# Expert logits computed with tokens on the partitions instead of with the tokens along the free axis

## The chip, the core and the metric

The kernel runs on one core of a Trainium2 chip. A core has five engines that run their own instruction streams and meet at semaphores: TensorE (PE: matrix products; its weight loads are listed apart as PEld), VectorE (DVE), ScalarE (ACT), GpSimd (POOL) and SyncE (SP, which issues the DMAs here). On-chip data lies in SBUF, 128 partitions wide; TensorE writes its products to PSUM, which the kernel uses as eight banks of 128 x 512 four-byte numbers, and DVE or ACT carry them on from there. The metric is the device time of one execution in microseconds; lower is better.

## What is computed

The input `x` is 16 sequences of 512 tokens with 256 channels. It is normalised, and the output is `x` plus a multi-query attention (16 heads of width 16, one shared key and value head) plus a mixture of six small experts, both of the normalised tokens. The change lies in the expert part. Cut to what matters, with `E = 6` experts, `L = 100` learned tokens each, rank `R = 16`, `C = 256` channels:

```python
logits = x @ w_gate                              # [n, E]
top_vals, top_idx = lax.top_k(logits, 1)
gates = zeros.at[arange(n)[:, None], top_idx].set(softmax(top_vals))
tokens = einsum('elr,erc->elc', A, B)            # [E, 100, C], rank 16
attn = einsum('nc,elc->nel', x, tokens) * C ** (-0.5)
attn = softmax(attn, axis=-1)                    # over the 100 learned tokens
val = einsum('elc,dc->eld', tokens, wt_w) + wt_b
delta_f = einsum('nel,eld->ned', attn[:, :, 1:], val[:, 1:, :])
delta = (einsum('ned,cd->nec', delta_f + x[:, None, :], wd_w) + wd_b) * scale[0]
combined = sum(exp(delta) * gates[:, :, None], axis=1)
out = feats + log(where(combined == 0, eps, combined))
```

One expert is open for a token (its gate is one), so the kernel computes only that one: the logits of a token against the 100 learned tokens of its own expert are `A_e (B_e x)`. `B x` for all six experts is 96 numbers a token (`ER = 96`); those of the five closed experts are multiplied by zero; and one product over the 96 rows with `A` then gives the 100 logits.

## The kernel before

The work is cut into 16 batches, one for each sequence (`NB = 16`, `T = 512` tokens). A batch's work is cut into some 310 jobs, each one method of the class `Batch`: `load`, `stats`, `norm`, `trans` (transposes of the normalised tokens), `q`, `e`, `kv` (projections), `amax` (a first pass over the attention logits that finds the maxima, on 128 x 512 tiles `pA`), `score`, `exp` and `pv` (the attention proper: logits `ps`, their exponentials `P`, the products `po`), `wo` (the output projection `py`) and the expert jobs. No order is left to a scheduler: each job has a written-out place in one of four tables (`FIRST`, `SECOND`, `MIDDLE` for batches 2 to 14, `LAST`), a batch's table is shifted by `PERIOD = 131072` units for each batch, all jobs of all batches are sorted by place (line 1175), and each engine executes its instructions in that order. So a place sets only who comes before whom, and the jobs of two or three batches are interleaved. `OTHER` and `KINDS` (lines 361 and 449) say which engine does a job.

PSUM banks come from a ring of eight (`Ring`, line 396): a job that makes a product takes the bank that has been free longest, and the job that reads it gives it back; TensorE must then wait until the bank's last reader is done.

Products that must be nearly exact in four bytes are made by `mm3` (line 424): each operand is split into a rounded part and the rest, both of type `float32r` (FR), and three products are accumulated: first with first (line 426), first with rest (427), rest with first (428). The first operand given to a product is the stationary one, which a weight load brings into the array; the second one is moved through it, one column after another.

The expert jobs that the change touches, in the order in which a batch executes them:

- `z` (line 674): `B x`, 96 rows by 512 tokens, in a bank `pz`; `z_ev` multiplies it by the mask of the open expert into `zu`; `z_split` splits it into the pair `self.Z`, two tiles of 96 x 512 (the profile calls them `F`).
- `s` (line 694): `mm3` with `aT` (the pair that holds the transposed `A`, 96 rows by 100 columns) as the stationary operand and `Z`, 512 columns wide, as the moving one. The 100 x 512 logits, tokens along the free axis, go to a bank `pS`.
- `s_ev` (line 698): ACT copies the bank to an SBUF tile `fs` in every batch (`KINDS` names ACT first for it and `OTHER` has no entry for it).
- `s_t` (line 704): four transposes of 100 x 128 of `fs` into one bank `pT`. The tokens then lie on the partitions, 100 logits in each quarter of the bank.
- `s_max` (line 709): DVE takes the maximum of the 100 logits of each token and subtracts it, reading `pT` twice; `s_exp` (716) on ACT, `p_t` (719) transposes back, `p_split`, `g` and the rest follow.

In a middle batch the places are `z_split` -152096, `s` -145485, `s_ev` -142958, `s_t` -137276, `s_max` -130921; between `s` and `s_t` stand jobs of other parts, among them `amax`, `score` and the eight transposes of the next tokens.

Of the kernel before, what the change touches and what calls it, by code (L numbers as in the profile page):

```python
# [8 lines left out]
F32 = mybir.dt.float32  # L9
# [59 lines left out]
    "z": -780943,  # L69
    "z_ev": -576470,  # L70
    "z_split": -548352,
    "s": -521686,
    "s_ev": -494550,
    "s_max": -431082,
    "s_exp": -359417,
    "p_split": -293663,
# [38 lines left out]
    "wo": (215817, 215842),  # L115
    "wo_ev": (216596, 217780),
    "store": 224560,
    "s_t": -481591,
    "p_t": -315138,
    "fin3": (40264, 22382),  # L120
    "fin4": (74229, 86847),
# [23 lines left out]
    "z": -324174,  # L145
    "z_ev": -309855,
    "z_split": -270323,
    "s": -218678,
    "s_ev": -209993,
    "s_max": -170106,  # L150
    "s_exp": -121203,
    "p_split": -114910,
# [37 lines left out]
    "wo": (177597, 177346),  # L190
    "wo_ev": (182932, 182876),
    "store": 185963,
    "s_t": -182999,
    "p_t": -116683,
    "fin3": (85629, 17491),
    "fin4": (103962, 139179),
# [23 lines left out]
    "z": -157899,  # L220
    "z_ev": -156539,
    "z_split": -152096,
    "s": -145485,
    "s_ev": -142958,
    "s_max": -130921,
    "s_exp": -125321,
    "p_split": -117179,
# [37 lines left out]
    "wo": (174065, 177554),  # L265
    "wo_ev": (176557, 183488),
    "store": 192519,
    "s_t": -137276,
    "p_t": -119609,
    "fin3": (74999, 108824),  # L270
    "fin4": (77905, 117792),
# [23 lines left out]
    "z": -158149,  # L295
    "z_ev": -154439,
    "z_split": -142977,
    "s": -125619,
    "s_ev": -123150,
    "s_max": -113232,  # L300
    "s_exp": -111784,
    "p_split": -87249,
# [46 lines left out]
    "tail_wo2": (2206909, 1942360, 2812099, 2282694),  # L349
    "tail_ev": (2218028, 1993855, 3175267, 2301583),  # L350
    "tail_store": (2237425, 2218212, 3336794, 2419839),
    "s_t": -118987,
    "p_t": -89378,
    "fin3": (390985, 455221),
    "fin4": (721831, 1298561),
# [18 lines left out]
def tile_kernel(ctx, tc, x, Wq, bq, Wkv, bkv, Wo, bo, A, B, w_gate, wt_w, wt_b, wd_w, wd_b, scale, out):  # L374
    nc = tc.nc
    ctx.enter_context(tc.manual_schedule())
    NB, T, C = x.shape
    E, L, R = A.shape
# [13 lines left out]
    sb2 = ctx.enter_context(tc.tile_pool(name="sb2", bufs=2))  # L392
# [29 lines left out]
    bank = banks.take  # L422

    def mm3(ps, a, b, first=True, last=True):
        (a1, a2), (b1, b2) = a, b
        nc.tensor.matmul(ps, a1, b1, start=first, stop=False)  # L426
        nc.tensor.matmul(ps, a1, b2, start=False, stop=False)  # L427
        nc.tensor.matmul(ps, a2, b1, start=False, stop=last)  # L428
# [10 lines left out]
    def split(engs, p1, p2, src):  # L439
        affine(engs[0], p1, src)  # L440
        engs[1].tensor_tensor(p2, src, p1.bitcast(F32), ALU.subtract)  # L441

    def at(pair, *idx):
        return (pair[0][idx], pair[1][idx])

    ALL = slice(None)
# [6 lines left out]
        ("p_split", (AV, VV, AV)),  # L453
        ("tail_split", (AV, VV, PV)),
        ("prep_kv prep_kv2", (nc.gpsimd, nc.vector, nc.vector)),
        ("trans_ev q_ev s_ev m_ev", (nc.scalar, nc.vector, nc.vector)),
        ("amax_ev", (nc.scalar, nc.vector, nc.vector)),
        ("e_ev ks_ev mask_ev o_ev tail_o", (nc.vector, nc.scalar, nc.scalar)),
    )
# [2 lines left out]
    def copy(eng, dst, src):  # L462
        (eng.copy if eng is nc.scalar else eng.tensor_copy)(dst, src)

    def cols(t, n=128):
        return slice(t * n, t * n + n)


    class Batch:
# [220 lines left out]
        def z_split(self):  # L690
            self.Z = self.pair(ER, "Z")
            split(self.eng("z_split"), self.Z[0], self.Z[1], self.zm)

        def s(self):
            p = self.pb[("s", 0)] = bank(f"pS{self.b}")
            mm3(p[:L], aT, self.Z)

        def s_ev(self):
            p = self.last(("s", 0))
            self.fs = self.tile(sb2, [L, T], F32, "fs")  # L700
            copy(self.eng("s_ev"), self.fs, p[:L])


        def s_t(self):
            p = self.pb[("st", 0)] = bank(f"pT{self.b}")
            for t in range(4):
                nc.tensor.transpose(p[:, t * 128 : t * 128 + L], self.fs[:, cols(t)], ident[:L, :L])

        def s_max(self):
            p = self.last(("st", 0)).rearrange("p (t l) -> p t l", t=4)[:, :, 0:L]  # L710
# [284 lines left out]
    ident = const.tile([128, 128], F32, name="ident")  # L995
# [7 lines left out]
    def fr_pair(shape, name):  # L1003
        return (const.tile(shape, FR, name=name + "1"), const.tile(shape, FR, name=name + "2"))
# [24 lines left out]
    aT = fr_pair([ER, L], "aT")  # L1029
# [174 lines left out]
```

## Time and profile before

| | |
|---|---|
| median of three runs | 927.23 us (926.7 to 928.15) |
| the profiled execution's own time | 929.27 us |
| its span, first to last instruction | 927.5 us |
| mean granted TensorE clock | 0.984 of full speed |

The profiled execution is one run with the profiler on. Its span is what the rows of the profile add up to; its own time is 1.8 us more, for what lies before the first and after the last instruction.

The rows of the groups that the change touches, summed over the span (a "busy" time counts each moment once; a mean is how long one instruction is in flight, and as products are pipelined, two that follow each other start closer together than that):

| instructions | engine | count | busy us | mean ns |
|---|---|---|---|---|
| products `pS<-F,aT` (lines 426, 427, 428) | PE | 16 each | 7.4, 6.2, 6.3 | 464, 389, 395 |
| copy `fs<-pS` 100 x 512 (line 463) | ACT | 16 | 9.4 | 591 |
| transposes `pT<-ident,fs` 100 x 128 (line 707) | PE | 64 | 8.6 | 258 |
| maximum `sm<-pT` 128 x 400 (line 712) | DVE | 16 | 9.1 | 566 |
| difference `es<-pT,sm` 128 x 400 (line 714) | DVE | 16 | 9.2 | 574 |

For comparison, the other products in `float32r` have 512 (`pq`, `pz`, `pG`, `pA`, `ps`), 294 (`pe`), 258 (`pM`) and 256 (`py`) moving columns, and the operands of the transposes (`pt`, `pk`, `pP`, `pT`, `pMt`) are four bytes wide with 100 or 128 moving columns.

### The profile page before, as it was taken

The page shows a single profiled execution, that of the slowest core. Times are in us where ns is not written, and L with a number is a line of the kernel's source. Part 1 is how long each engine was busy: PE and PEld are TensorE (multiplying, and loading weights), DVE is VectorE, ACT ScalarE, POOL GpSimd, SP SyncE. Part 2 cuts the span into 40 slices and gives each one's busy share as a digit, 9 for nine tenths or more (in the row PEclk, how much of TensorE's full clock was granted, in tenths as well). Part 3 has the DMA queues.
Part 4 walks back from the last instruction along what each step waited for, and adds up shares of the span by engine and source line. Part 5 has one row for each costly group of instructions (what it writes and reads, how often), then busy time and mean ns, then how long its engine had stood idle before and what let it go on. Part 6 is the DMA issues. An engine that isn't in the chain of part 4 may idle for free.

```text
span 927.5 us, 18665 instructions
## 1 busy us (share of the span) xinstructions
PE 913.6 (99%) x5994; PEld 483.4 (52%) x5997; DVE 792.0 (85%) x2049; ACT 777.4 (84%) x1715; POOL 613.7 (66%) x842
## 2 busy tenths in 40 slices
PE   8999999999999999999999999999999999999997
PEld 5655445555645555554545555454555545444443
DVE  6798898899898999989898998989888888887743
ACT  4688878889899888989898888989888898897775
POOL 3484746767677776767767676776767677465364
PEclk9989999999999999999999999999999999999989
DMA  3311122231213223131322313132231312222001
GB/s 105 92 36 34 51 49 71 56 77 50 71 40 82 59 68 76 44 71 44 72 59 72 72 44 73 42 72 58 71 73 42 72 43 51 59 51 69 27 26 36
DMA packets 92253, 54.74 MB, mean 59 GB/s; under 512 B 19323, under 2 KB 88188, under 8 KB 92156
## 3 DMA queue, kind: packets, MB, share of 16 engines
q1 hardware_dynamic: 92156, 53.55, 23.3%
q8 instruction: 48, 0.79, 0.4%
q14 instruction: 49, 0.40, 0.1%
HBM read 17.89 MB, written 8.90 MB: 29 GB/s over the span
## 4 chain that ended last, share of the span: by engine, by line
PE 90%; DVE 4%; DMA 2%; ACT 1%; issue 1%; POOL 1%; SPq 0%; POOLq 0%; ACTq 0%; DVEq 0%
PE po L837 26%; PE pA L782 17%; PE ps L821 17%; PE pe L426 2%; PE py L426 2%; PE pq L426 2%; PE pe L428 2%; PE pe L427 2%; PE pq L427 2%; PE py L428 2%; PE pq L428 2%; PE py L427 2%; PE pt L559 1%; DVE rl L795 1%; PE pk L654 1%; DVE M L797 1%
## 5 line engine op out<-in xcount | busy, mean ns | idle before, releaser
L829 ACT ACTIVATE P<-ps 128x512 f32<-128x512 f32 x1024 | 547.5, 614 | 63.4 <-PE ps L821 59.4
L797 DVE TENSOR_REDUCE M<-pA 128x1 f32<-128x512 f32 x661 | 428.6, 683 | 55.3 <-PE pA L782 47.8
L837 PE MATMUL po<-P,vt 128*32 128x512 f32 x2048 | 265.0, 603 | 0.1
L821 PE MATMUL ps<-qst,kst 50*128 50x512 f32 x1024 | 227.7, 443 | 2.5 <-DMA qst<-mt 0.9
L782 PE MATMUL pA<-kst,qst 48*128 48x512 f32 x1024 | 216.6, 444 | 1.4 <-DVE es L714 0.6
L821 PEld LDWEIGHTS ps<-qst,kst 50*128 50x128 f32 x1024 | 108.2, 186 | 114.6 <-DVE M L795 20.5
L782 PEld LDWEIGHTS pA<-kst,qst 48*128 48x128 f32 x1024 | 100.9, 187 | 119.5 <-ACT P L829 20.6
L794 ACT ACTIVATE rl<-pA 128x256 f32<-128x256 f32 x363 | 129.1, 392 | 35.7 <-PE pA L782 32.3
L795 DVE CUSTOM_DVE_ANT_0 rl<-pA,rl 128x256 f32<-128x256 f32 x363 | 141.1, 418 | 20.9 <-ACT rl L794 19.3
L837 PEld LDWEIGHTS po<-P,vt 128*32 128x32 f32 x2048 | 45.0, 108 | 92.5 <-issue 69.7
L758 POOL TENSOR_SCALAR g<-dl 128x512 f32<-128x512 f32 x32 | 61.7, 1930 | 34.7 <-DVE dl L750 33.2
L880 POOL TENSOR_TENSOR oq<-ao,rb 128x512 f32<-128x512 f32 x31 | 40.2, 1298 | 58.8 <-DMA rb<-dr 26.7
L441 POOL TENSOR_TENSOR F<-zu,F 96x512 fp32r<-96x512 f32 (+1 forms) x32 | 41.0, 1281 | 15.1 <-ACT F L433 11.4
L764 POOL TENSOR_SCALAR dl<-dl 128x512 f32<-128x512 f32 x32 | 47.8, 1492 | 2.4
L437 POOL TENSOR_SCALAR F<-zu 98x512 fp32r<-98x512 f32 (+1 forms) x29 | 18.4, 635 | 45.7 <-DVE zu L688 42.5
L441 POOL TENSOR_TENSOR qs<-qf,qs 128x512 fp32r<-128x512 f32 x32 | 41.2, 1288 | 10.9 <-ACT qs L433 8.6
L765 POOL TENSOR_TENSOR w<-dl,w 128x512 f32<-128x512 f32 x32 | 41.2, 1289 | 2.7
L426 PE MATMUL pe<-e1w,X 128*128 128x294 f32 x128 | 41.9, 327 | 0.0
L441 POOL TENSOR_TENSOR O<-oq,O 128x512 fp32r<-128x512 f32 x31 | 39.8, 1285 | 2.5
L769 POOL TENSOR_TENSOR g<-g,bob 128x512 f32<-128x512 f32 x32 | 41.1, 1284 | 0.2
L773 POOL TENSOR_TENSOR w<-g,w 128x512 f32<-128x512 f32 x32 | 41.1, 1287 | 0.1
L635 POOL TENSOR_TENSOR oh<-e,mx 128x24 f32<-128x24 f32 x16 | 3.7, 231 | 55.2 <-ACT P L829 37.5
(209 smaller groups left out, 1503.6 us busy)
## 6 DMA issues: line engine op xcount, KB each, us to landing
qst<-qs SPq DMA_DIRECT2D x384, 64.0 KB
rb<-dr SPq DMA_DIRECT2D x31, 256.0 KB
xt<-in_L_attn_x SPq DMA_DIRECT2D x15, 512.0 KB
out<-y SPq DMA_DIRECT2D x15, 512.0 KB
qst<-mt SPq DMA_DIRECT2D x128, 8.0 KB
dc<-os SPq DMA_DIRECT2D x62, 8.0 KB
dr<-dc SPq DMA_DIRECT2D x62, 8.0 KB
xt<-in_L_attn_x SPq DMA_DIRECT2D x4, 128.0 KB
```

What stands on the lines that cost most here:

```text
L426: nc.tensor.matmul(ps, a1, b1, start=first, stop=False)
L427: nc.tensor.matmul(ps, a1, b2, start=False, stop=False)
L428: nc.tensor.matmul(ps, a2, b1, start=False, stop=last)
L441: engs[1].tensor_tensor(p2, src, p1.bitcast(F32), ALU.subtract)
L758: nc.gpsimd.tensor_scalar(self.g1[:, two], self.dl[:, two], EXP_ZERO, LOG_EPS - EXP_ZERO, ALU.is_lt, ALU.mult)
L782: nc.tensor.matmul(p, self.qst[g][rows, h], self.kst[rows, keys], start=True, stop=True)
L794: nc.scalar.activation(rl, p[:, HT:], AF.Relu)
L795: nc.vector.tensor_tensor_reduce(rl, p[:, 0:HT], rl, 1.0, NEG, ALU.add, ALU.max, accum_out=mx)
L797: nc.vector.tensor_reduce(mx, p, AX.X, ALU.max)
L821: nc.tensor.matmul(p, self.kst[rows, cols(c)], self.qst[hp // 4][rows, :, cols(hp % 4, 32)], start=True, stop=True)
L829: nc.scalar.activation(self.P_[k][:, u], banks.give(self.ps.pop(i)), AF.Exp)
L837: nc.tensor.matmul(self.po[n][32 * j : 32 * j + 32], lv, self.P_[2 * w + j // 2][:, j % 2], start=c == 0, stop=c == 3)
```

## The change

`s` and `s_t` become one job that keeps the name `s` and stands at the places that `s_t` had. For each quarter of the tokens it makes the same three products with the operands exchanged: 128 columns of `Z` are now the stationary operand, and `aT`, 100 columns wide, is the moving one. The result has the tokens on the partitions and is written straight to where the transposes put it, so `s_max` and all that follows is as before. `s_ev`, its copy, the tile `fs`, the bank `pS` and the transposes are gone. `Z` is read later than before: at the place of `s_t`.

```diff
@@ the four tables; here MIDDLE @@
-    "s": -145485,
-    "s_ev": -142958,
+    "s": -137276,
...
-    "s_t": -137276,
@@ KINDS @@
-        ("trans_ev q_ev s_ev m_ev", (nc.scalar, nc.vector, nc.vector)),
+        ("trans_ev q_ev m_ev", (nc.scalar, nc.vector, nc.vector)),
@@ class Batch @@
         def s(self):
-            p = self.pb[("s", 0)] = bank(f"pS{self.b}")
-            mm3(p[:L], aT, self.Z)
-
-        def s_ev(self):
-            p = self.last(("s", 0))
-            self.fs = self.tile(sb2, [L, T], F32, "fs")
-            copy(self.eng("s_ev"), self.fs, p[:L])
-
-
-        def s_t(self):
             p = self.pb[("st", 0)] = bank(f"pT{self.b}")
             for t in range(4):
-                nc.tensor.transpose(p[:, t * 128 : t * 128 + L], self.fs[:, cols(t)], ident[:L, :L])
+                mm3(p[:, t * 128 : t * 128 + L], at(self.Z, ALL, cols(t)), aT)
```

The places in the other three tables change in the same way (`FIRST` -521686 to -481591, `SECOND` -218678 to -182999, `LAST` -125619 to -118987).

More of the change, by code (lines that the diff above doesn't have):

```diff
@@ L71 @@
     "z_split": -548352,
-    "s": -521686,
-    "s_ev": -494550,
+    "s": -481591,
     "s_max": -431082,
@@ L117 @@
     "store": 224560,
-    "s_t": -481591,
     "p_t": -315138,
@@ L147 @@
     "z_split": -270323,
-    "s": -218678,
-    "s_ev": -209993,
+    "s": -182999,
     "s_max": -170106,
@@ L192 @@
     "store": 185963,
-    "s_t": -182999,
     "p_t": -116683,
@@ L297 @@
     "z_split": -142977,
-    "s": -125619,
-    "s_ev": -123150,
+    "s": -118987,
     "s_max": -113232,
@@ L351 @@
     "tail_store": (2237425, 2218212, 3336794, 2419839),
-    "s_t": -118987,
     "p_t": -89378,
```

## The prediction

> **What bounds the kernel now.** I read the page's busy times first, then the chain of work that ended last, then the costliest groups with their idle time, then stretches of one batch each.
>
> ```profile
> PE 913.6 (99%) x5994; PEld 483.4 (52%) x5997; DVE 792.0 (85%) x2049; ACT 777.4 (84%) x1715; POOL 613.7 (66%) x842
> ...
> PE 90%; DVE 4%; DMA 2%; ACT 1%; issue 1%; POOL 1%; SPq 0%; POOLq 0%; ACTq 0%; DVEq 0%
> ...
> L829 ACT ACTIVATE P<-ps 128x512 f32<-128x512 f32 x1024 | 547.5, 614 | 63.4 <-PE ps L821 59.4
> L797 DVE TENSOR_REDUCE M<-pA 128x1 f32<-128x512 f32 x661 | 428.6, 683 | 55.3 <-PE pA L782 47.8
> L837 PE MATMUL po<-P,vt 128*32 128x512 f32 x2048 | 265.0, 603 | 0.1
> L821 PE MATMUL ps<-qst,kst 50*128 50x512 f32 x1024 | 227.7, 443 | 2.5 <-DMA qst<-mt 0.9
> L782 PE MATMUL pA<-kst,qst 48*128 48x512 f32 x1024 | 216.6, 444 | 1.4 <-DVE es L714 0.6
> ```
>
> TensorE is busy 99% and is 90% of the chain. Busy products alone would prove little, since their ends are modelled; the other side does: ACT idles 63.4 us ahead of the exponentials, nearly all until a product `ps` comes, DVE 55.3 us ahead of the maxima, until a `pA` comes, while the three large groups of products had 0.1, 2.5 and 1.4 us of idle time before them. In stretches of about one batch:
>
> ```profile
> 361.00:414.50 53.50, 53.50 (x372) 28.38 (x368) 48.37 (x125) 47.44 (x105) 39.08 (x54) 1.00 0.26 63
> 414.50:468.20 53.70, 53.70 (x370) 28.34 (x368) 48.29 (x125) 47.37 (x105) 39.04 (x54) 1.00 0.26 62
> ```
>
> The columns are the stretch, its length, then busy us and count of PE, PEld, DVE, ACT and POOL, and the granted clock. TensorE has no idle moment in it at full clock; DVE has some 5 us to spare in 53.5, ACT 6, POOL 14. So the change is worth what it does to TensorE's own stream, sixteen times, and the copy that it takes from ACT is worth nothing as long as TensorE stays the last.
>
> **What it takes from TensorE.** For products, the price is the distance from one start to the next. Here is the stream around both jobs in a middle batch (start in us, time in flight, then what; rows of one group are merged, with their count):
>
> ```profile
> 437.11 0.38 PE L654 MATMUL pk<-ident,kp 128*128 128x128 f32 x2
> 437.24 0.47 PE L426 MATMUL pS<-F,aT 96*100 96x512 f32 x1
> 437.56 0.39 PE L427 MATMUL pS<-F,aT 96*100 96x512 f32 x1
> 437.78 0.40 PE L428 MATMUL pS<-F,aT 96*100 96x512 f32 x1
> 438.11 0.73 PE L782 MATMUL pA<-kst,qst 48*128 48x512 f32 x4
> 438.68 0.40 PE L821 MATMUL ps<-qst,kst 50*128 50x512 f32 x2
> 439.01 1.09 PE L559 MATMUL pt<-ident,xn 128*128 128x128 f32 x8
> 439.94 0.51 PE L707 MATMUL pT<-ident,fs 100*128 100x100 f32 x4
> 440.23 0.36 PE L426 MATMUL pM<-mw,F 98*128 98x258 f32 x1
> 440.43 0.28 PE L427 MATMUL pM<-mw,F 98*128 98x258 f32 x1
> 440.55 0.29 PE L428 MATMUL pM<-mw,F 98*128 98x258 f32 x1
> 440.76 0.51 PE L821 MATMUL ps<-qst,kst 50*128 50x512 f32 x2
> ```
>
> The wide products: `pA` starts at 438.11. Without `pS` it would follow `pk`, whose second transpose starts 0.11 after the first, at 437.22; from a full-array product to the next attention pair the stream needs 0.21 (`pM` 440.55 to `ps` 440.76), so `pA` could start at 437.43. The three wide products hold TensorE for 438.11 - 437.43 = 0.68 us.
>
> The transposes: from 439.94 to `pM` at 440.23 are 0.29; that `pM` needs 0.20 to its second product against 0.12 for the next step is a first weight load that shows, another 0.08. That is 0.37 us for four. Taken away: 1.05 us a batch, 16.8 us in all.
>
> **What it adds to TensorE.** Four quarters with three products: twelve instructions, each with its own load of 128 weight columns (the page counts one load for each product, 5997 for 5994, and repeats one also where two following products have the same stationary operand: lines 426 and 427 of `pS` loaded it 16 times each). Each moves 100 columns. No product in `float32r` of this kernel has fewer than 256 moving columns, so the price of one is bounded from rows on both sides:
>
> - Below, by the 16-bit products `pm` of 128 moving columns: four of them take 0.24 us from 29.03 to the next product at 29.27, 0.06 each. Twelve are 0.72 us, that is -0.33 a batch and -5.3 us.
> - By the weight load. `pyT`, four-byte products of 96 moving columns with 128 weight columns:
>
> ```profile
> 21.44 1.03 PE L1121 MATMUL pyT<-scr_O,scr_g 128*128 128x96 f32 x8
> 22.30 1.03 PE L1017 MATMUL warm<-scr_O 128*128 128x512 bf16 x4
> ```
>
>   Eight starts take 0.86 us: 0.107 each. The wide `float32r` rows with new weights each time come no closer either: 0.12 for 258 columns (`pM`, 440.43 to 440.55). Twelve at 0.107 to 0.12 are 1.28 to 1.44 us: +0.23 to +0.39 a batch, +3.7 to +6.2 us.
> - By the rate of narrow four-byte columns. `pT` moves 100 columns in one pass in 0.085 (its second to fourth instruction start at 440.03, 440.11 and 440.20 in the trace), 0.85 ns a column; `pt` 128 columns in 0.11; both are near twice the 0.46 ns a column of `pM`. A transpose needs one such pass, an exact product two: `pyT` is four products in the code and eight instructions in the profile. Two passes of 100 columns are 0.17. Twelve at 0.17 to 0.18 are 2.04 to 2.16 us.
> - Above, by `pyT` taken whole: two instructions, 0.215 a product. Twelve are 2.58 us: +1.53 a batch, +24.5 us.
>
> I take 0.175: the row nearest in width and in bytes is `pyT`, every four-byte row below 256 columns pays the double price for a column, and the single price is seen only at 256 columns and above. The doubled load of `pyT` I leave out, as one instruction will do one load. Then 12 x 0.175 = 2.10, less 1.05, is +1.05 us a batch and **+16.8 us** in sixteen.
>
> The page "TensorE: Matmul & The Clock Gate" of the Trainium skill, section "Back-to-back issue gap", speaks against this: pairs of a weight load and a product with 128 columns sustain about 81 ns. By it twelve would take 0.97 us and the change would save 0.08 a batch, 1.3 us in all. But `pyT`, narrower, took 0.107 here, and the page's weight-load section gives columns over 1.2 as ns, 107 for 128, which is that number; I expect four-byte weights to stay at it at best.
>
> **What it moves, and who hides it.** ACT loses sixteen copies of 0.591, 9.4 us, and the ring one of its takers a batch: both lie under TensorE's stream, so they count nothing; were ACT the pace, they would be the whole gain. The later reading of `Z` costs nothing: its second part is written by POOL in the row 434.82 to 436.10, and the new job starts near 439.3. No DMA is issued or passed. On TensorE the attention products, `pM` and all else queue behind the twelve. On DVE, `rd` and `dl` (lines 749, 750), which read `pM`, stand ahead of `sm` and `es`, and the maxima of the attention behind them. `pM` ended at 440.84 and `rd` began at 441.77; with the stream 0.68 earlier and the new job 1.73 longer, `pM` ends at 441.89, so DVE may stand for 0.1 to 0.8 us. Its 5 us to spare a batch hide that; without them it would be up to 0.8 x 16 = 13 us. ACT gets no new scores for the length of the job and has 6 us to spare.
>
> **The sum.** The span of 927.5 and the median of 927.2 differ by less than the runs do, so I add to the median: 927.2 + 16.8 = **944.0 us**, 1.8% slower. The price of 0.16 to 0.19 gives 941 to 947 for this case alone.
>
> **The rivals.**
>
> - *The weight load decides.* If `float32r` keeps its 0.46 ns a column at 100 columns, the moving takes 0.046 and the load of 128 columns hides it and sets 0.107 to 0.12: 931 to 933.5 us. For it speaks that these instructions are single ones, unlike `pyT`; against it, that no four-byte row below 256 columns shows the single rate.
> - *The other side: ACT sets the pace.* The copies are 9.4 us of ACT, and TensorE's weight loads wait for ACT's releases in many short waits (those of `ps` and `pA` for `P`, 20.3 and 20.6 us in total). If these waits, and not the array, space the products, each copy removed lets a bank go 0.59 us sooner: 927.2 - 9.4 + 3.7 for the cheap price of the new products = 921.5. It decides once the twelve cost under 1.05 + 0.59 = 1.64 us, 0.137 each, and ACT is last. Against it: TensorE has no idle moment in a middle batch, ACT has six.
> - *Twice the load and a DVE that stands.* 0.215 a product gives 951.7, and with DVE's stand uncovered more.
> - *Nothing to measure.* Savings on both sides cancel: the price of 0.088 each, below any four-byte row.
>
> **How the numbers follow.** A measurement of this kernel can tell about 0.2%, 1.9 us, from no change. Forecast 0.57; weight load 0.25; ACT or the 16-bit price, both faster, 0.07; nothing 0.04; doubled 0.07. Faster 0.07, same 0.04, slower 0.89. The range takes in the forecast's 941 to 947 and the weight-load rival from 931, and a little on both sides for waits at the start and the end, where clock and order differ: 929 to 948. It leaves out the faster cases, no change and the doubled price, 0.18.
>
> **What the changed profile would show.** Twelve `pT` products in three groups at lines 426 to 428, 100 moving columns, no `fs` and no line 707 or its like. Right: from the first of them to `pM` some 2.1 us, a batch period near 54.6 us, ACT and DVE with more idle time ahead of `ps` and `pA`, TensorE still without idle time. Wrong: a distance of 0.107 to 0.12 (the first rival), a period shorter than 53.5 us (ACT was the pace), or idle TensorE behind `rd`, `sm` or a bank. The clock is a risk of its own: it was granted at 0.91 in the stretch from 40 to 94 us, and a changed start could lengthen or shorten that by a few us.

## The result and the profile after

The changed kernel takes 935.81 us (median of four runs, 935.17 to 936.38) against 927.69 us for the kernel before in the same series: ratio 1.0083, 95% interval 1.0068 to 1.0099. It is slower by about 8 us, half of what was forecast. The profiled execution took 935.78 us with a span of 934.0, 6.5 us more than the span before. The page of the changed kernel, busy times, chain and the large groups (its line numbers are smaller by 8 at `mm3` and by 17 from `s_max` on):

```profile
PE 920.0 (99%) x6074; PEld 491.8 (53%) x6077; DVE 792.6 (85%) x2049; ACT 771.9 (83%) x1699; POOL 612.5 (66%) x842
...
PE 79%; DVE 6%; POOL 5%; DMA 3%; issue 3%; ACT 2%; SPq 1%; POOLq 0%; DVEq 0%
...
L812 ACT ACTIVATE P<-ps 128x512 f32<-128x512 f32 x1024 | 547.0, 613 | 78.5 <-PE ps L804 75.5
L804 PE MATMUL ps<-qst,kst 50*128 50x512 f32 x1024 | 226.6, 443 | 1.4 <-DVE ao L846 0.5
L765 PE MATMUL pA<-kst,qst 48*128 48x512 f32 x1024 | 218.4, 445 | 0.7
```

TensorE is still the busy engine, and ACT now idles 78.5 us ahead of the exponentials instead of 63.4: the copies that it lost became waiting for products. The chain has less of TensorE than before, but the large groups of products wait as little as before for anything that the page shows as idle time.

The stream of TensorE around the change, in the same batch as the prediction's (start, time in flight, what):

```profile
440.37 0.38 PE L646 MATMUL pk<-ident,kp 128*128 128x128 f32 x2
440.68 0.86 PE L765 MATMUL pA<-kst,qst 48*128 48x512 f32 x4
441.37 0.41 PE L804 MATMUL ps<-qst,kst 50*128 50x512 f32 x2
441.86 1.16 PE L551 MATMUL pt<-ident,xn 128*128 128x128 f32 x8
442.78 0.29 PE L418 MATMUL pT<-aT,F 96*128 96x100 f32 x1
442.91 0.28 PE L419 MATMUL pT<-aT,F 96*128 96x100 f32 x1
443.02 0.27 PE L420 MATMUL pT<-aT,F 96*128 96x100 f32 x1
443.13 0.28 PE L418 MATMUL pT<-aT,F 96*128 96x100 f32 x1
...
444.13 0.35 PE L418 MATMUL pM<-mw,F 98*128 98x258 f32 x1
444.32 0.29 PE L419 MATMUL pM<-mw,F 98*128 98x258 f32 x1
444.45 0.28 PE L420 MATMUL pM<-mw,F 98*128 98x258 f32 x1
444.65 0.50 PE L804 MATMUL ps<-qst,kst 50*128 50x512 f32 x2
```

Read against the stream before, start to start. From `pk` to `pA` it is 0.31 us instead of 1.00: the wide products are gone, -0.69. The narrow products follow each other at 0.11; from the first to `pM` it is 1.35 us instead of 0.29, +1.06. And between them something that the prediction did not have: from `pA` to `ps` 0.69 instead of 0.57, from `ps` to `pt` 0.49 instead of 0.33, together +0.28 for the very same instructions. All in all from `pk` to the last `ps` 4.28 instead of 3.65 us.

Where the first 0.12 of these 0.28 go, the weight loads and ACT show (the kernel after; in brackets the idle time before an instruction and what ended it):

```profile
440.68 0.19 PEld L765 LDWEIGHTS pA<-kst,qst 48*128 48x128 f32 x2 [0.17 <-ACT P L812]
441.03 0.19 PEld L765 LDWEIGHTS pA<-kst,qst 48*128 48x128 f32 x2 [0.17 <-ACT P L812]
```

```profile
438.92 2.07 ACT L812 ACTIVATE P<-ps 128x512 f32<-128x512 f32 x4 [0.26 <-PE ps L804]
```

The load of the second `pA` pair starts at 441.03, together with its product, instead of some 0.1 us behind the first pair's as before. ACT's four exponentials end at 438.92 + 2.07 = 440.99: the pair needed a bank that one of them had just emptied. The order in which the kernel hands out its banks says the same: the pair's first product takes the bank that the last of the four exponentials reads. TensorE comes to this pair 0.69 us sooner, ACT does not.

The other 0.16, ahead of `pt`, are a wait for a bank too:

```profile
441.83 0.42 PEld L551 LDWEIGHTS pt<-ident,xn 128*128 128x128 f32 x4 [0.38 <-POOL w L756]
```

```profile
441.43 0.28 DVE L791 SCALAR_TENSOR_TENSOR mt<-pMt,mt 32x128 fp32r<-32x128 f32 x1
```

The releaser named is on POOL, but none of POOL's instructions in this kernel reads a bank, and `xn`, which POOL made, was done at 439.90. By the kernel's order `pt` takes the bank of `pMt`, where it took that of `pS` before. DVE's second `mt` empties it at 441.43 + 0.28 = 441.71, and in ten middle batches on end the load of `pt` starts 0.115 to 0.116 us behind the end of this `mt`. That end comes 1.34 us behind the start of `pk` in both kernels: DVE, too, is no sooner, while TensorE now is.

A batch's period, from one `sm` on DVE to the next, shows the sum: 53.4 to 53.5 us before from the fourth to the eighth batch (counted from 0), 54.0 after in three of these four; in the other, 54.36, TensorE also idles 0.31 us ahead of a `po`. That is +0.55, and 16 x 0.55 = 8.8 us. The spans differ by less, above all since the kernel before loses more in its six later middle batches (periods of 53.7 to 54.7, against 54.0 to 54.8 after): there the two differ by 1.1 us in all and not by 6 x 0.55 = 3.3. One place, in the trace of the kernel before:

```profile
496.31 0.40 PE L821 MATMUL ps<-qst,kst 50*128 50x512 f32 x1
497.17 0.47 PE L821 MATMUL ps<-qst,kst 50*128 50x512 f32 x1 [0.47 <-DMA qst<-mt]
```

The score products of the next batch wait there for the DMA that carries the maxima `mt` into `qst`. TensorE idles 0.47 us here, and 0.18 and 0.27 in two later batches, for this DMA; in a fourth it is 0.69 at the same pair, where the trace names `es` on DVE. In the profile after, the same pair starts without a gap in the middle batches. I read it so that behind a stream that is 0.63 us longer the pair comes when the maxima have landed; no run tests this.

### The profile page after: what moved, and what is told of

It is laid out like the page before. It is cut to its first block, busy times and chain, and to the rows that moved or that the text cites. A ratio compares the mean times of both kernels' runs of the same rounds, so it can differ in the third digit from the quotient of the medians.

```text
span 934.0 us, 18815 instructions
## 1 busy us (share of the span) xinstructions
PE 920.0 (99%) x6074; PEld 491.8 (53%) x6077; DVE 792.6 (85%) x2049; ACT 771.9 (83%) x1699; POOL 612.5 (66%) x842
## 4 chain that ended last, share of the span: by engine, by line
PE 79%; DVE 6%; POOL 5%; DMA 3%; issue 3%; ACT 2%; SPq 1%; POOLq 0%; DVEq 0%
PE po L820 23%; PE pA L765 15%; PE ps L804 14%; PE pe L418 2%; DVE rl L778 2%; DVE M L780 2%; PE pt L551 2%; PE py L418 2%; PE pq L418 2%; PE pe L420 2%; PE pe L419 2%; PE py L420 2%; DMA rb<-dr 2%; PE pq L420 1%; PE pq L419 1%
## 5 line engine op out<-in xcount | busy, mean ns | idle before, releaser
L812 ACT ACTIVATE P<-ps 128x512 f32<-128x512 f32 x1024 | 547.0, 613 | 78.5 <-PE ps L804 75.5
L418 PE MATMUL py<-wo,O 128*128 128x256 f32 x128 | 38.9, 304 | 1.5 <-POOL O L429 0.7
```

What stands on the lines that cost most here:

```text
L812: nc.scalar.activation(self.P_[k][:, u], banks.give(self.ps.pop(i)), AF.Exp)
```

## The experiments

All are made from the changed kernel, in two series on two chips, each with the kernel before beside them: `e2_wide`, `e4_two`, `e6_copy` and `e1d` with a median of 928.53 us for it, the others with 929.34. Ratios are to these; that of the changed kernel itself, to compare with, is 1.0083. "Period" is that of middle batches without an extra wait, 53.96 to 54.05 us for the changed kernel. The diffs leave out the entries of the tables where a job is put at the places of a removed one.

**What sets the price of a narrow product: the moving columns?** `e2_wide` (the tile `aT` is made twice as wide, too):

```diff
-            for t in range(4):
-                mm3(p[:, t * 128 : t * 128 + L], at(self.Z, ALL, cols(t)), aT)
+            for t in range(4):
+                w = 2 * L if t < 3 else L
+                mm3(p[:, t * 128 : t * 128 + w], at(self.Z, ALL, cols(t)), (aT[0][:, 0:w], aT[1][:, 0:w]))
```

> The changed kernel with the moving operand made 200 columns wide (two copies of the 100 logit columns) in three of the four quarters; the second 100 columns are overwritten by the next quarter. Theory W (the load of 128 weight columns sets the distance of 0.112 us, and the moving columns go at the single rate of about 0.45 ns and are hidden under it): 200 columns are 0.09 us, the distance stays at 0.11 to 0.12, the time within 1.5 us of the changed kernel's 935.8. Rival D (narrow four-byte columns do cost double, 0.085 us for 100, just hidden under the load): the distance goes to about 0.17 for nine of twelve products, +0.5 us a batch, +8.5 us, 944.

Ratio 1.0075 (1.006 to 1.009), 935.86 us, period 53.96 to 54.05. The stream:

```profile
442.63 0.34 PE L418 MATMUL pT<-aT,F 96*128 96x200 f32 x1
442.80 0.28 PE L419 MATMUL pT<-aT,F 96*128 96x200 f32 x1
442.91 0.28 PE L420 MATMUL pT<-aT,F 96*128 96x200 f32 x1
443.03 0.27 PE L418 MATMUL pT<-aT,F 96*128 96x200 f32 x1
443.14 0.28 PE L419 MATMUL pT<-aT,F 96*128 96x200 f32 x1
...
443.59 0.28 PE L420 MATMUL pT<-aT,F 96*128 96x200 f32 x1
443.70 0.22 PE L418 MATMUL pT<-aT,F 96*128 96x100 f32 x1
443.76 0.28 PE L419 MATMUL pT<-aT,F 96*128 96x100 f32 x1
443.87 0.28 PE L420 MATMUL pT<-aT,F 96*128 96x100 f32 x1
```

200 moving columns cost 0.11 us like 100: at most 0.56 ns a column. Had four-byte columns below 256 cost the 0.85 ns of the transposes, it would be 0.17. Only the first step is 0.17 long, where it is 0.13 in the changed kernel, and the step behind the first product with 100 columns is 0.06 instead of 0.11; the whole group takes 1.36 us as before. So 100 columns more move a start by 0.04 to 0.05 us, about 0.45 ns a column and not 0.85. This shows that the double price, from which the forecast was made, isn't there.

**Or the weight columns?** `e9_half` adds twelve products with half the weight columns to the same place:

```diff
+            half = bank(f"pH{self.b}", 0)
+            for t in range(4):
+                mm3(half[0:64, t * 128 : t * 128 + L], at(self.Z, ALL, cols(2 * t, 64)), aT)
```

> The changed kernel with twelve more products a batch, as the new ones but with 64 weight columns instead of 128, into a bank that nobody reads. Theory W (the load of the weight columns sets the distance of the new products): the additional ones follow each other at about 0.056 to 0.07 us, 0.7 to 0.8 us a batch, 946.5 to 949. Rival M (something else sets 0.112, the moving columns or a fixed price of an instruction): 0.112 again, 1.34 us a batch, 957.

Ratio 1.0169 (1.0149 to 1.0189), 945.48 us, 1 us below what was expected; period 54.6 to 54.8. The twelve take 0.70 us in the stream. Old and new kind stand side by side in its stream:

```profile
451.22 0.28 PE L419 MATMUL pT<-aT,F 96*128 96x100 f32 x1
451.34 0.28 PE L420 MATMUL pT<-aT,F 96*128 96x100 f32 x1
451.45 0.22 PE L418 MATMUL pH<-aT,F 96*64 96x100 f32 x1
451.51 0.22 PE L419 MATMUL pH<-aT,F 96*64 96x100 f32 x1
451.56 0.22 PE L420 MATMUL pH<-aT,F 96*64 96x100 f32 x1
```

The same 100 moving columns, 64 weight columns instead of 128, and the distance falls from 0.112 to 0.058 us. The weight load sets it, for these products. The page "TensorE: Matmul & The Clock Gate" of the Trainium skill, section "LDWEIGHTS (loading the stationary operand)", gives columns over 1.2 in ns, 107 and 53; these products agree, with some 5 ns on top. Not every row does: the transposes `pT` of the kernel before have 128 weight columns as well and start 0.085 us apart, below the page's 107 ns; there the measurement decides, and 0.112 is not the price of every load of 128 columns. The page's 81 ns for a pair of load and product, from its section "Back-to-back issue gap", did not come about here.

**Is TensorE's stream the pace?** `e4_two` takes one of the three products away, `e6_copy` gives ACT its copies back:

```diff
-                mm3(p[:, t * 128 : t * 128 + L], at(self.Z, ALL, cols(t)), aT)
+                (z1, z2), (a1, a2) = at(self.Z, ALL, cols(t)), aT
+                ps = p[:, t * 128 : t * 128 + L]
+                nc.tensor.matmul(ps, z1, a1, start=True, stop=False)
+                nc.tensor.matmul(ps, z2, a1, start=False, stop=True)
```

> The changed kernel without the product of the first part of Z with the rest of A: eight products a batch instead of twelve, the logits lose that term. Theory W (TensorE's stream is what counts, 0.112 us a product): 4 x 0.112 = 0.45 us a batch less, 7.2 us, 928.6. Rival B (what the change cost beyond the sum is waits for PSUM banks, and these set the pace around the job): part of it turns into longer waits, 930 to 933. Rival A (ACT or DVE is the pace): 935.

Ratio 1.0012 (0.9996 to 1.0029), 929.56 us, period 53.5 to 53.6. The ten runs lie from 925.98 to 933.04, so that the time alone does not tell theory W from rival B; the period does. The group of narrow products went from 1.358 to 0.912 us, 0.446 less for four products, and the period fell by about as much, 0.4 to 0.5: nothing of it was eaten by waits.

```diff
+        def s_ev(self):
+            fs = self.tile(sb2, [ER, T], F32, "fs")
+            nc.scalar.copy(fs, self.zm)
```

> The changed kernel with sixteen copies on ACT given back (96 x 512 from zu to a tile that nobody reads) at the places of the removed ones. Theory W (the removed copies were hidden under TensorE): within 1.5 us of 935.8. Rival A (ACT sets the pace, and the removal of 9.4 us of copies hid a larger loss on TensorE): up to 945.

Ratio 1.0069 (1.0054 to 1.0084), 935.27 us. Its busy line:

```profile
PE 919.1 (98%) x6074; PEld 491.3 (53%) x6077; DVE 791.7 (85%) x2049; ACT 776.6 (83%) x1715; POOL 612.1 (66%) x842
```

ACT runs sixteen copies again (1715 instructions, as before the change), 0.63 us each where the removed ones took 0.59, and the time does not rise. The removed copies waited for a product, these do not. The removal of the copy was worth nothing, and ACT is not the pace.

**The 0.28 us between `pk` and the narrow products.** Do the pairs wait because TensorE comes sooner, or because the ring of banks, one taker short, gives them other banks? `e3_ring` takes and gives back a bank where the old `s` stood, `e5_plus_wide` also makes the wide products there, into a bank that nobody reads:

```diff
+        def s_ring(self):
+            banks.give(bank(f"pS{self.b}"))
```

> The changed kernel with one bank taken from the ring and given back at the place of the old s, without any instruction: every later job then gets the bank that it had before the change. Theory T (TensorE comes to the attention pairs behind pk 0.69 us sooner, while ACT and DVE give the banks back when they did before; so it waits there whatever bank it gets): the waits of about 0.26 us a batch stay or grow, 935 to 938. Rival R (the ring's shift by one gives these pairs banks that come free later): they go, 932.

Ratio 1.0059 (1.0039 to 1.008), 935.08 us, period 53.95 to 54.09: no change. From `pk` to the first narrow product it is 2.42 us, 2.41 in the changed kernel, so the shift of the ring by one is not the cause. The edit does less than was expected of it: the bank comes back at once and not when ACT has copied it, so the next products down to `pt` still take other banks than in the kernel before, `pt` that of `pMt`. That no choice of banks would help is not shown.

```diff
+        def s_wide(self):
+            p = bank(f"pS{self.b}", 0)
+            mm3(p[:L], aT, self.Z)
```

> The changed kernel with the three wide products of the old s made again at their old place, into a bank that nobody reads. By their own length they cost 0.69 us a batch. Theory T (they covered waits for banks of about 0.26 us a batch): the middle batch grows by 0.42 only, from 54.0 to 54.45 us, 942.5. Rival S (no waits that they could cover): 54.7 us, 946.8.

Ratio 1.0123 (1.0103 to 1.0143), 941.31 us. The period is 54.36 to 54.44 in five middle batches, +0.33 to +0.41 for products that are 0.69 long, and 54.7 to 55.1 in others, with further waits. The time says the same: 6.2 us more than `e3_ring` in the same series, 0.39 a batch. The stream:

```profile
447.95 0.38 PE L650 MATMUL pk<-ident,kp 128*128 128x128 f32 x2
448.09 0.47 PE L422 MATMUL pS<-F,aT 96*100 96x512 f32 x1
448.40 0.39 PE L423 MATMUL pS<-F,aT 96*100 96x512 f32 x1
448.63 0.40 PE L424 MATMUL pS<-F,aT 96*100 96x512 f32 x1
448.95 0.73 PE L773 MATMUL pA<-kst,qst 48*128 48x512 f32 x4
449.52 0.41 PE L812 MATMUL ps<-qst,kst 50*128 50x512 f32 x2
449.86 1.09 PE L555 MATMUL pt<-ident,xn 128*128 128x128 f32 x8
450.70 0.29 PE L422 MATMUL pT<-aT,F 96*128 96x100 f32 x1
```

From `pA` to `ps` it is 0.57 again, from `ps` to `pt` 0.34, and `pt` takes 0.84 instead of 0.92. `pt` takes the bank of `pMt` here as well, and does not wait for it. The wide products of the kernel before were about half free: while they ran, ACT and DVE emptied banks that TensorE had to wait for otherwise.

**Can something useful cover the waits?** `e1d` makes the narrow products where the wide ones stood, in batches 2 to 14, and reads them sooner, since the ring of eight has no bank to spare for longer:

```diff
-    "s": -137276,
+    "s": -145485,
...
-    "s_max": -130921,
+    "s_max": -140890,
```

> The changed kernel with the job s of batches 2 to 14 at the place where the wide products stood, straight behind the transposes pk, and s_max earlier too, so that the bank is held no longer. Theory B (of the 0.55 us a middle batch that the change cost, about 0.27 are waits for banks which arose because nothing stands any more between pk and the attention pairs behind it): these go, the middle batch falls from 54.0 to about 53.75 us, 932.3. Rival S (no waits, but the price of the twelve products themselves or of their switches): the period stays at 54.0, 935.8 within 1.

A miss: ratio 1.0168 (1.0142 to 1.0194), 943.57 us, period 54.6 to 54.7. The waits that were meant went as expected (from `pA` to `ps` 0.57 again), but larger ones took their place. Its weight loads, and DVE:

```profile
445.66 0.86 PEld L551 LDWEIGHTS pt<-ident,xn 128*128 128x128 f32 x8 [0.78 <-DVE M L780]
...
447.44 0.19 PEld L804 LDWEIGHTS ps<-qst,kst 50*128 50x128 f32 x2 [0.53 <-DVE es L697]
```

```profile
444.92 0.69 DVE L780 TENSOR_REDUCE M<-pA 128x1 f32<-128x512 f32 x1 [0.82 <-PE pA L765]
...
446.21 0.57 DVE L695 TENSOR_REDUCE sm<-pT 128x4 f32<-128x400 f32 x1
446.81 0.57 DVE L697 TENSOR_TENSOR es<-pT,sm 128x400 f32<-128x400 f32 x1
```

DVE stood idle for 0.82 us while TensorE made the narrow products ahead of `pA`. Its maximum `M` then ended at 445.61 only, and by the kernel's order the bank that it read is the one that `pt` takes. The `ps` at 447.44 takes the bank of the narrow products themselves, which `es` empties at 446.81 + 0.57 = 447.38. `e7_fill` put the fourth `pM` of the batch before, and its reading by DVE, behind `pk` instead:

```diff
-    "d": (-41643, -39645, -39091, -5887),
-    "d_ev": (-38957, -37390, -33557, -1639),
+    "d": (-41643, -39645, -39091, -14300),
+    "d_ev": (-38957, -37390, -33557, -11800),
```

> The changed kernel with the fourth product pM of the batch before (and the DVE work that reads it) moved from behind the new products to the place behind pk, in batches 2 to 14: useful work where the wide products stood, no new switch between full-array products and attention pairs. Theory T: the waits of pA and pt for banks shrink by what it covers, 0.2 to 0.26 us a batch, 53.75 to 53.85 us, 932 to 933.5. Rival S: 935.8 within 1. Should DVE's work, now earlier, hold banks elsewhere, as sm and es did when they were moved, it gets slower than 936.

A miss too: ratio 1.0093 (1.0071 to 1.0116), 939.07 us, 4 us more than `e3_ring` in the same series, period 54.2 to 54.3 where it is shortest. The pairs run without waits, and `pt` pays for it:

```profile
441.89 0.73 PE L765 MATMUL pA<-kst,qst 48*128 48x512 f32 x4
442.47 0.66 PE L804 MATMUL ps<-qst,kst 50*128 50x512 f32 x2
443.31 1.22 PE L551 MATMUL pt<-ident,xn 128*128 128x128 f32 x8 [0.19 <-POOL qs L429]
```

From `pA` to `ps` it is 0.58, but from `ps` to `pt` 0.84. The releaser named there is a split on POOL, none of whose instructions in this kernel reads a bank, so it was another. By the kernel's order `pt` takes here a bank of the first `pA` pair, which a maximum `M` on DVE reads from 442.50 to 443.17; in eleven batches on end the load of `pt` starts 0.115 to 0.116 us behind the end of that `M`. So an order that is better for the narrow products has not been found, and no version here beats the kernel before: the nearest, `e4_two`, lacks a term and is level with it.

## Why the prediction was right and wrong

- *TensorE's stream sets the time, ACT's copy is worth nothing.* Right: `e6_copy` and `e4_two` show both sides of it. The rival in which ACT is the pace is out.
- *What the change takes away.* The 0.68 us for the wide products was measured as 0.69. Of the 0.37 for the transposes 0.08 was wrong: I took the first step of `pM`, 0.20, for a cost of the transposes in front, but it is 0.19 behind the narrow products as well. 0.29 is gone.
- *What it adds: the step that failed.* I took 0.175 us for a narrow product, "the rate of narrow four-byte columns", 2.10 a batch. It is 0.112, and 1.35 a batch, 0.75 x 16 = 12 us too much. I had read the double price of the transposes and of `pyT` as one of narrow four-byte columns. `e2_wide` shows that it isn't: `float32r` moves 200 columns within 0.112. What the runs put in its place is the load of 128 weight columns (`e9_half`). `pyT` had shown that number: its 0.107 is a mean of eight steps, of which seven are 0.111 to 0.112. The rival that took it had the right price.
- *The bank ring counts nothing.* Wrong, by 0.28 us a batch at this place. I priced the removed products by their length; they also covered waits for banks (`e5_plus_wide`). So the weight-load rival's 931 to 933.5 was too low. The measured 935.8 lies between the two cases that the stated range joins, and in neither.
- *The later `Z`, and DVE behind `pM`.* Right: no product waits for `Z`, and DVE runs from the casts of `X` through `rd` to `es` without an idle moment in the batch shown.
- *No DMA is issued or passed.* Wrong in later batches: the kernel before waits there for the landing of `mt`, 0.18 to 0.47 us in three batches, and the changed one shows no such wait in its middle batches. That its longer stream is the reason is argued and not tested.

With measured terms: -0.69 + 1.06 + 0.28 is +0.65 at the place; the steps of `pt` and `pM` give back 0.02 and a step further on some 0.1: about +0.55 a batch, 8.8 us in sixteen, of which the later batches give back some 2. The spans say 6.5, the medians 8.1.

## What to carry to other kernels

Turning a product round so that its result lands transposed makes the wide operand the weights: count the weight columns first, since here each of the twelve loads of 128 columns cost 0.112 us whether 100 or 200 columns moved, and twelve of them cost more than three wide products and four transposes. Sixteen copies on an engine that isn't the pace were worth nothing here, to remove or to put back. And an instruction in the stream of the pacing engine may be half free because others catch up behind it: price its removal by when the next instructions get their buffers, not by its length.

## What the runs showed of the hardware

A `float32r` product with 128 new weight columns follows the one before at 0.112 us with 100 as with 200 moving columns, and at 0.058 us with 64 weight columns. Narrow `float32r` products do not pay the 0.85 ns a column that the four-byte transposes pay in this trace. These transposes, in turn, start 0.085 us apart with 128 weight columns each, closer than the products' 0.112.
